# Cross-attention block: pair 4's turns back in step 4, norm1's turn of pair 3 at the end of step 5, the last pair's transfers on two queues, the last residual on VectorE

## The chip, the cores and the metric

The kernel runs on one core of a Trainium2 chip. The time is the device time of one execution in microseconds; lower is better. A core has five engines with queues of their own, which work in order: TensorE (PE in the profile; its weight loads are PEld), VectorE (DVE), ScalarE (ACT), GpSimd (POOL) and SyncE (SP). SP here does nothing but issue DMA transfers; ScalarE can issue some too. An engine waits for another, or for a transfer, on semaphores.

## The reference

A transformer block with strictly causal cross-attention, over 128 batches of 128 tokens, model width 256, 16 heads of 16, hidden width 1024, all in float32:

```python
q = (x @ Wq + bq);  k = (c @ Wk + bk);  v = (c @ Wv + bv)      # 16 heads of 16
scores = q @ k.T / sqrt(16);  allowed = j < i                   # strictly below the diagonal
attn = softmax(where(allowed, scores, -1e30));  attn[row 0] = 0
x1 = layer_norm(x + (attn @ v) @ Wo + bo, ln1_g, ln1_b)
out = layer_norm(x1 + relu(x1 @ W1 + b1) @ W2 + b2, ln2_g, ln2_b)
```

## The kernel before, in words

Two batches form a pair p, 0 to 63. The order on every engine is written out by hand: the kernel calls small functions, each of which records the instructions of one piece of work, and each engine runs its instructions in the order in which they were recorded. Software pipelining is done in this text. A step p holds the scores and the softmax of pair p, and beside them later stages of earlier pairs. `third()`, `fourth()`, `fifth()` and `fall_in(5)` are written out for p = 2, 3, 4, 5; `step(p)` serves 6 to 63; `behind(62)`, `behind(63)` and the lines after them empty the pipeline. Step numbers here are pair numbers.

The pieces that the change and the prediction name, with the lines of the kernel before:

- `scores_both` (L376) puts the scores in all eight PSUM banks; `mask` (L390), `mask_high` (L743, L747) and `low_maximum` (L754) run on VectorE, the exponentials on ScalarE (L762). `sums` adds up the rows on VectorE (L421) and multiplies by the reciprocals on GpSimd (L423).
- `turn(p, hi, t)` (L436) is a transpose of 32 x 32 blocks on VectorE, three for each pair: two for the upper half of the queries (hi = 1, t = 0 and 1) and one for the lower. They fill the tile tb. `bring` (L451) then moves tb's blocks to their places in the tile pT with 16 transfers of 96 KB; each of them reads what all three turns wrote. `LATE_FIRST` is the order of the 16.
- `weigh(p)` (L483, L493) multiplies pT with the values, into bank 7 (pc); `context` (L505) copies that out on ScalarE; `attention_out` (L512) multiplies with Wo; `attention_sum` (L538), `attention_stats` (L525, L526; L532, L533 on GpSimd), `shift` (L577) and `norm1` (L554, ScalarE) make x1.
- `turn_x1(p)` turns x1: a transpose on VectorE (L663) into tbx, then four transfers to DRAM (L239) and one back (L242) into x1T.
- `hidden(p)` (L699) multiplies x1T with W1 in four parts of two chunks; ScalarE applies the ReLU after each part (L707), and a function may be called between the parts. `residual1(p)` (L566, L569) makes x1b, the residual of the second half, on GpSimd.
- `combine_hidden` (L780 to L783) and `second_by_seven` (L794) multiply with W2 in seven products of quarter size instead of eight, into banks 6 and 7 (py, pz); `sum_of_seven` (L823, L831) adds them up with x1b on VectorE and frees the banks. Pairs 0 and 1 use `second` (L719) with `second_sum` (L729), pair 2 `second_half` (L840, sum L846).
- `norm2` (L591, ScalarE), `finish` (L597, L598, GpSimd) and `store` (L606, SP) end a pair; its tile t2 has two buffers, so that the sum of pair p waits for the store of pair p - 2.
- `load_ahead` issues the loads of x and c of coming pairs on SP (L92, L99).

In step p TensorE runs weigh(p - 2), scores(p), queries(p + 1), attention_out(p - 2), keys(p + 1), values(p), the product with W2 of pair p - 4 and hidden(p - 3). So step 6 begins with weigh(4), has second_half(2, 1) in the place of the product with W2, and ends with hidden(3).

Before the change, the first turn of pair 4 stands at the end of `fifth()`, its other two turns and the transfers in `fall_in(5)`, behind all masks of pair 5; on SP the store of pair 0 and the loads of `load_ahead(5)` stand ahead of those transfers. Pair 5 has its first two turns at the end of `fall_in(5)` and its third in step 6. `turn_x1(3)` stands in step 6 behind the third turn and the transfers of pair 5, on VectorE as on SP. In step 63, SP issues all 16 transfers of pair 63 and then store(58).

Of the kernel before, what the change touches and what calls it, by code (L numbers as in the profile page):

```python
# [19 lines left out]
def tile_cross_attention_block(  # L20
# [22 lines left out]
    nc = tc.nc  # L43
# [6 lines left out]
    FC = DFF // P  # L50
# [3 lines left out]
    NP = B // 2  # L54
# [162 lines left out]
    def bank(name):  # L217
        turns[0] += 1
        return at_bank(4 + turns[0] % 4, name)
# [210 lines left out]
    def turn(p, hi, t):  # L430

        st = states[p]
        if "tb" not in st:
            st["tb"] = wide(f"tb_{p}").rearrange("p (j n) -> p j n", j=NS)
        at = (t if hi else 2) * 256
        nc.vector.transpose(  # L436
            st["tb"][:, :, at : at + 256].rearrange("p j (n a) -> p n j a", a=32),
            st["sm", hi].rearrange("p h j -> p (h j)")[:, t * 1024 : (t + 1) * 1024].rearrange(
                "p (n j a) -> p n j a", j=NS, a=32
            ),  # L440
        )

    def bring(p, queue, which):

        st = states[p]
        if "pT" not in st:
            pT = st["pT whole"] = wide(f"pT_{p}").rearrange("p (i n) -> p i n", i=NS)
            st["pT"] = pT.rearrange("p i (n a) -> p i n a", a=32)
        for u in which:
            i, j = u // NS, u % NS  # L450
            queue.dma_start(  # L451
                st["pT whole"][32 * j : 32 * j + 32, i, :], st["tb"][32 * i : 32 * i + 32, j, :]
            )
# [49 lines left out]
    def context(p):  # L503
        pc = states[p].pop("pc").rearrange("p (u i) -> p u i", i=P)
        nc.scalar.copy(cxT.rearrange("p m s i -> p (m s) i")[:, :, 1:], pc[:, :, 1:])  # L505
# [53 lines left out]
                x1[:, s], t1[:, s], mv[:, s, 0:1], sd[:, s], ALU.subtract, ALU.mult  # L559
            )  # L560

    def residual1(p):

        st = states[p]
        x1b = st["x1b"] = ffn.tile([P, 2, D], F32, tag="x1b", name=f"x1b_{p}", bufs=3)
        nc.gpsimd.tensor_tensor(  # L566
            x1b, st["x1"], g1_r[:, None, :].to_broadcast([P, 2, D]), ALU.mult
        )
        nc.gpsimd.tensor_tensor(  # L569
            x1b, x1b, be1b_r[:, None, :].to_broadcast([P, 2, D]), ALU.add  # L570
        )

# [115 lines left out]
    def hidden(p, fs, between=None, banks=(2, 3, 4, 0)):  # L688
        st = states[p]
        if fs[0] == 0:  # L690
            st["hT"] = ffn.tile([P, FC, TP], F32, tag="hT", name=f"hT_{p}", bufs=1)
        for f in fs[::2]:
            if p == 0:
                ph = bank(f"ph_{p}_{f}")
            else:
                ph = at_bank(banks[f // 2], f"ph_{p}_{f}")
            for i in range(2):
                for k in range(KC):
                    nc.tensor.matmul(  # L699
                        ph[:, i * TP : (i + 1) * TP].rearrange("p (s i a) -> p s i a", s=2, a=32),  # L700
                        w1[:, k, (f + i) * P : (f + i + 1) * P], st["x1T"][:, :, :, k, :],
                        start=(k == 0), stop=(k == KC - 1),
                    )
                    if p == 1:
                        empty(3 if f else 2)
            for i in range(2):
                nc.scalar.activation(  # L707
                    st["hT"][:, f + i, :], ph[:, i * TP : (i + 1) * TP], AF.Relu,
                    bias=(b1e_c if p else b1_c)[:, f + i : f + i + 1], scale=1.0,
                )  # L710
            if between:
                between(f)
# [277 lines left out]
    EVERY = range(NS * NS)  # L990
# [52 lines left out]
    LATE_FIRST = (*EVERY[8:], *EVERY[:8])  # L1043
# [44 lines left out]
    def fifth():  # L1088
        p = 4
        load_ahead(p)  # L1090
        scores_both(p)
        mask(p, 0, B)
        mask(p, 1, A)
        maximum(p, 1, ONE)
        queries(p + 1)
        mask(p, 1, B)
        maximum(p, 1, TWO)
        exponential(p, 1, ONE)
        mask(p, 0, A)
        maximum(p, 0, ALL)  # L1100
        keys(p + 1)
        exponential(p, 1, TWO)
        values(p)
        values_out(p)
        sums(p, 1, ONE)
        exponential(p, 0, ALL)
        sums(p, 1, TWO)
        sums(p, 0, ALL)
        tokens(p + 2, "x")
        tokens(p + 2, "c")  # L1110
        second(1, 0)
        second(1, 1)
        combine_w2()
        turn(p, 1, 0)
        hidden(2, range(FC // 2))

    ONES, TWOS = range(HH), range(HH, H)
# [2 lines left out]
    def fall_in(p):  # L1120

        weigh(p - 2)
        context(p - 2)
        scores_both(p)
        second_sum(1)
        finish(0)
        store(0)
        add_bo(p - 1)
        residual1(2)
        load_ahead(p)  # L1130
        mask(p, 0, B)
        mask_high(p, A)
        exponential_by_head(p, 1, ONES)
        mask_high(p, B)
        exponential_by_head(p, 1, TWOS)
        mask(p, 0, A)
        low_maximum(p)
        turn(p - 1, 1, 1)
        turn(p - 1, 0, 0)
        bring(p - 1, nc.sync, LATE_FIRST)  # L1140
        queries(p + 1)
        exponential_by_head(p, 0, ONES)
        attention_out(p - 2)
        attention_sum(p - 2)
        attention_stats(p - 2)
        shift(p - 2, 1)
        project_keys(p + 1)
        values(p)
        sums(p, 1, ONE)
        sums(p, 1, TWO)  # L1150

        def between(f):
            if f == 4:
                exponential_by_head(p, 0, TWOS[:4])

        hidden(2, range(FC // 2, FC), between, (2, 3, 2, 3))
        exponential_by_head(p, 0, TWOS[4:])
        copy_keys(p + 1)
        values_out(p)
        norm1(p - 2)  # L1160
        tokens(p + 2, "x")
        tokens(p + 2, "c")
        turn(p, 1, 0)
        sums(p, 0, ALL)
        turn(p, 1, 1)
        second_half(2, 0)
        stats(1, states[1]["t2"], 2)
        scale_and_shift(1)

    def step(p):  # L1170
        last = p == NP - 1
        weigh(p - 2)
        context(p - 2)
        scores_both(p)
        if p > 6:
            combine_hidden(p - 4, POOL_ALONE)
        add_bo(p - 1)
        load_ahead(p)
        mask(p, 0, B)
        if last:  # L1180
            mask(p, 0, A)
        mask_high(p, A)
        exponential_by_head(p, 1, ONES)
        mask_high(p, B)
        exponential_by_head(p, 1, TWOS)
        if not last:
            mask(p, 0, A)
        low_maximum(p)
        exponential_by_head(p, 0, range(H))
        if p == 6:  # L1190
            turn(p - 1, 0, 0)
            bring(p - 1, nc.sync, LATE_FIRST)
            turn_x1(p - 3)
        if not last:
            queries(p + 1)
        attention_out(p - 2)
        attention_sum(p - 2)
        attention_stats(p - 2)
        shift(p - 2, 1)
        norm1(p - 2)  # L1200
        if not last:
            keys(p + 1)
        values(p)
        values_out(p)
        norm2(p - 5)
        sums(p, 1, ONE)
        sums(p, 1, TWO)
        sums(p, 0, ALL)
        turn_x1(p - 2)
        residual1(p - 3)  # L1210
        if p > 6:
            second_by_seven(p - 4)
        else:
            second_half(2, 1)
        hidden(p - 3, range(FC))
        if p + 2 < NP:
            tokens(p + 2, "x")
            tokens(p + 2, "c")
        turn(p, 1, 0)
        if p > 6:  # L1220
            sum_of_seven(p - 4)
        turn(p, 1, 1)
        turn(p, 0, 0)
        bring(p, nc.sync, LATE_FIRST)
        finish(p - 5)
        store(p - 5)
        stats(p - 4, states[p - 4]["t2"], 2)
        scale_and_shift(p - 4)
# [10 lines left out]
    def behind(p):  # L1239

        weigh(p)
        context(p)
        combine_hidden(p - 2, VECTOR_ALONE)
        norm2(p - 3)
        finish(p - 3)
        store(p - 3)
        second_by_seven(p - 2)
        attention_out(p)
        attention_sum(p)
        attention_stats(p)  # L1250
        shift(p, 1)
        residual1(p - 1)
        sum_of_seven(p - 2)
        stats(p - 2, states[p - 2]["t2"], 2)
        scale_and_shift(p - 2)
        hidden(p - 1, range(FC), lambda f: norm1(p) if f == 0 else None)
        turn_x1(p)

    p = NP - 1
# [1 line left out]
    behind(p - 1)  # L1261
    behind(p)
    combine_hidden(p - 1, VECTOR_ALONE)
    norm2(p - 2)
    second_by_seven(p - 1)
    residual1(p)
    finish(p - 2)
    store(p - 2)
    sum_of_seven(p - 1)
    hidden(p, range(FC))  # L1270
    stats(p - 1, states[p - 1]["t2"], 2)
    deviation(p - 1, 2)
    for s in range(2):
# [57 lines left out]
```

## Time and profile before

| what | us |
| --- | --- |
| median of 3 runs | 1552.5 (1551.95 to 1552.52) |
| the profiled execution | 1554.08 |
| its span, first to last instruction | 1552.4 |
| TensorE busy | 1518.0 (98%) |
| VectorE busy | 1334.9 (86%) |
| GpSimd busy | 1261.0 (81%) |
| ScalarE busy | 1121.2 (72%) |
| transfers | 204.24 MB, mean 132 GB/s |

The rows quoted in the prediction are of these kinds. A timeline row gives the start and the length in us, the engine, the line of the kernel, the operation, what it writes and reads, the shape and how many instructions are merged; in brackets stand the idle time of that engine just before, and what ended it. PE is a matmul; SPq and ACTq are transfers being issued by SP and by ScalarE. A row of waits gives who waited for whom, the sum in us, how often, and the longest. A row of stretches gives the busy time of each engine in a stretch of the span, and the granted clock of TensorE as a share of full speed. A row of the chain of work that ended last gives start, length and what ran.

### The profile page before, as it was taken

What the parts mean: (1) busy time and instruction counts of PE and PEld (TensorE: products, weight loads), DVE (VectorE), ACT (ScalarE), POOL (GpSimd) and SP (SyncE); (2) the same over time, 40 slices, a digit from 0 to 9 for tenths busy, and PEclk for the clock granted to TensorE, in tenths of its full rate; (3) what the DMA queues carried; (4) which work ended last, traced back from release to release, by engine and by line L of the source; (5) the groups of instructions that cost most, each with busy time, mean ns of one, the idle gap of its engine ahead of it and who ended that gap; (6) DMA issues with size and microseconds to landing.
All of it is one profiled execution on the core that took longest, in us unless ns stands there. A gap on an engine that the chain in (4) does not pass through costs nothing.

```text
span 1552.4 us, 47881 instructions
## 1 busy us (share of the span) xinstructions
PE 1518.0 (98%) x17926; PEld 1361.9 (88%) x17926; DVE 1334.9 (86%) x2496; ACT 1121.2 (72%) x3391; POOL 1261.0 (81%) x1284
## 2 busy tenths in 40 slices
PE   8995999999999999999999999999999999999998
PEld 7784898998998998998998998998998998998887
DVE  7987698898898898898898898898898898898875
ACT  5665587787787787787787787787787787787652
POOL 6875688888888888888888888888888888888873
PEclk9997999999999999999999999999999999999999
DMA  8445565565565565565566565566565566564431
GB/s 195 93 95 119 122 142 133 132 141 143 135 138 132 131 149 139 131 141 136 130 143 145 130 140 129 135 142 147 130 140 134 130 142 145 133 140 114 114 102 48
DMA packets 415285, 204.24 MB, mean 132 GB/s; under 512 B 282448, under 2 KB 383056, under 8 KB 415056
## 3 DMA queue, kind: packets, MB, share of 16 engines
q1 hardware_dynamic: 413152, 200.13, 56.1%
q8 instruction: 144, 2.36, 0.7%
q10 hardware_dynamic: 1904, 1.06, 0.3%
q14 instruction: 85, 0.70, 0.2%
HBM read 70.26 MB, written 33.29 MB: 67 GB/s over the span
## 4 chain that ended last, share of the span: by engine, by line
PE 92%; DVE 4%; DMA 2%; SPq 1%; issue 1%; ACT 1%; POOL 0%; ACTq 0%; POOLq 0%; DVEq 0%
PE ph L699 28%; PE py L794 13%; PE pz L794 10%; PE pq L261 7%; PE po L512 7%; PE pv L301 7%; PE pk L261 6%; PE pss L376 6%; PE pc L493 4%; PE pc L483 2%; SPq L451 1%; DVE su L421 1%; DMA x1T<-x1t 0%; PE py L719 0%; DMA pT<-tb 0%
## 5 line engine op out<-in xcount | busy, mean ns | idle before, releaser
L699 PE MATMUL ph<-x1T,w 128*128 128x256 f32 x2048 | 455.3, 380 | 12.8 <-DMA x1T<-x1t 12.7
L699 PEld LDWEIGHTS ph<-x1T,w 128*128 128x128 f32 x2048 | 385.4, 191 | 64.4 <-issue 13.2
L423 POOL TENSOR_TENSOR sm<-sm,rs 128x1024 f32<-128x1024 f32 x192 | 359.5, 1899 | 3.6 <-DVE rs L422 2.1
L707 ACT ACTIVATE hT<-ph,b1e_c 128x256 f32<-128x256 f32 x504 | 210.1, 469 | 189.2 <-PE ph L699 184.5
L762 ACT ACTIVATE sm<-pss,nmx 128x128 f32<-128x128 f32 x944 | 250.5, 416 | 127.3 <-DMA pT<-tb 85.2
L762 ACT ACTIVATE sm<-sm,nmx 128x64 f32<-128x64 f32 x944 | 232.2, 337 | 4.3
L390 DVE TENSOR_TENSOR sm<-pss,neg 128x256 f32<-128x256 f32 (+1 forms) x276 | 108.1, 434 | 146.6 <-PE pss L376 143.9
L421 DVE TENSOR_REDUCE su<-sm 128x8 f32<-128x1024 f32 (+1 forms) x192 | 225.8, 1176 | 3.9 <-ACT sm L409 3.8
L436 DVE STREAM_TRANSPOSE tb<-sm 128x1024 f32<-128x1024 f32 x186 | 221.1, 1214 | 0.0
L532 POOL TENSOR_SCALAR ve<-mv 128x2 f32<-128x2 f32 x127 | 28.9, 228 | 210.4 <-DVE mv L526 210.1
L794 PE MATMUL py<-wt,hS 128*128 128x128 f32 x1440 | 171.1, 275 | 1.0 <-DVE hS L782 0.5
L794 PEld LDWEIGHTS py<-wt,hS 128*128 128x128 f32 x1440 | 165.8, 192 | 1.4 <-DVE hS L782 0.7
L747 DVE TENSOR_REDUCE nmx<-pss 128x4 f32<-128x512 f32 x236 | 150.7, 680 | 0.0
L261 PE MATMUL pq<-xT,wq 128*128 128x256 f32 x504 | 125.4, 392 | 0.5 <-DVE sm L390 0.5
L291 ACT ACTIVATE kT<-pk,bkh,half 128x256 f32<-128x256 f32 x252 | 120.6, 559 | 3.9 <-PE pk L261 3.9
L512 PE MATMUL po<-wo,cxT 128*128 128x256 f32 x512 | 121.3, 380 | 0.7 <-ACT cxT L505 0.7
L301 PE MATMUL pv<-wv,cT 128*128 128x256 f32 x512 | 121.0, 379 | 0.0
L261 PE MATMUL pk<-cT,wk 128*128 128x256 f32 x504 | 119.2, 379 | 0.0
L512 PEld LDWEIGHTS po<-wo,cxT 128*128 128x128 f32 x512 | 96.9, 190 | 14.4 <-ACT cxT L505 1.2
L261 PEld LDWEIGHTS pq<-xT,wq 128*128 128x128 f32 x504 | 90.7, 189 | 20.8 <-issue 9.9
L301 PEld LDWEIGHTS pv<-wv,cT 128*128 128x128 f32 x512 | 97.2, 190 | 13.2
L261 PEld LDWEIGHTS pk<-cT,wk 128*128 128x128 f32 x504 | 95.7, 190 | 13.1 <-issue 0.2
(133 smaller groups left out, 2976.7 us busy)
## 6 DMA issues: line engine op xcount, KB each, us to landing
pT<-tb SPq DMA_DIRECT2D x984, 96.0 KB
x1t<-tbx SPq DMA_DIRECT2D x252, 64.0 KB
x1T<-x1t SPq DMA_DIRECT2D x63, 256.0 KB
out_dram<-t SPq DMA_DIRECT2D x63, 256.0 KB
xb<-in_x_dram SPq DMA_DIRECT2D x124, 128.0 KB
cb<-in_ctx_dram SPq DMA_DIRECT2D x124, 128.0 KB
x<-in_x_dram SPq DMA_DIRECT2D x31, 512.0 KB
w<-in_L_xattn_W_dram SPq DMA_DIRECT2D x2, 1024.0 KB
```

Source lines behind the costliest of these rows:

```text
L261: nc.tensor.matmul(ps[:, m * TP : (m + 1) * TP], w[:, k, m * P : (m + 1) * P], src[:, k, :], start=(k == 0), stop=(k == KC - 1),)
L291: nc.scalar.activation(st["kT"][:, m, e, :], pk[:, m * TP : (m + 1) * TP], AF.Identity, bias=bkh[:, m, e : e + 1], scale=half[:, e : e + 1],)
L301: nc.tensor.matmul(pv[:, s * D : (s + 1) * D], st["cT"][:, k, s * P : (s + 1) * P], wv[:, k, :], start=(k == 0), stop=(k == KC - 1),)
L421: nc.vector.tensor_reduce(su, sm[:, part, :], AX.X, ALU.add)
L423: nc.gpsimd.tensor_tensor(sm[:, part, :], sm[:, part, :], rs[:, :, None].to_broadcast([P, part.stop - part.start, n]), ALU.mult,)
L436: nc.vector.transpose(st["tb"][:, :, at : at + 256].rearrange("p j (n a) -> p n j a", a=32), st["sm", hi].rearrange("p h j -> p (h j)")[:, ...
L512: nc.tensor.matmul(po[:, s * D : (s + 1) * D], cxT[:, k, s, :], wo[:, k, :], start=(k == 0), stop=(k == KC - 1),)
L699: nc.tensor.matmul(ph[:, i * TP : (i + 1) * TP].rearrange("p (s i a) -> p s i a", s=2, a=32), w1[:, k, (f + i) * P : (f + i + 1) * P], st[ ...
L707: nc.scalar.activation(st["hT"][:, f + i, :], ph[:, i * TP : (i + 1) * TP], AF.Relu, bias=(b1e_c if p else b1_c)[:, f + i : f + i + 1], sc ...
L747: nc.vector.tensor_reduce(st["nmx", 1][:, 4 * r : 4 * r + 4], st["sps", 1][r].rearrange("p (n j) -> p n j", j=P), AX.X, ALU.max, negate=True,)
L762: nc.scalar.activation(sm[:, h, :], src, AF.Exp, bias=nmx[:, h : h + 1], scale=1.0)
L794: nc.tensor.matmul(out, left(k), right(k), start=(k == 0), stop=(k == FC // 2 - 1))
```

## The change

Four things, all of them order, queue or engine; the computation is the same.

1. The second and third turn of pair 4 and its 16 transfers move from `fall_in(5)` to `fifth()`, behind the first turn.
2. `turn_x1(3)` moves from the middle of step 6 to `fall_in(5)`, behind the second turn of pair 5 and ahead of `second_half(2, 0)`.
3. Of the 16 transfers of pair 63, the first eight of the order stay with SP in step 63; the other eight are issued by ScalarE in `behind(62)`, after `context(62)`.
4. `residual1(63)` runs on VectorE. `sum_of_seven(62)` follows it at once, `norm2(61)` is called after the first part of `hidden(63)`, and `finish(61)` and `store(61)` come after `hidden(63)`.

In the built program the sequence of matmuls on TensorE is the same before and after.

```diff
-    def residual1(p):
+    def residual1(p, engine=nc.gpsimd):
...
-        nc.gpsimd.tensor_tensor(
+        engine.tensor_tensor(
             x1b, st["x1"], g1_r[:, None, :].to_broadcast([P, 2, D]), ALU.mult
         )
-        nc.gpsimd.tensor_tensor(
+        engine.tensor_tensor(
             x1b, x1b, be1b_r[:, None, :].to_broadcast([P, 2, D]), ALU.add
         )
...
         turn(p, 1, 0)
+        turn(p, 1, 1)
+        turn(p, 0, 0)
+        bring(p, nc.sync, LATE_FIRST)
         hidden(2, range(FC // 2))
...
         low_maximum(p)
-        turn(p - 1, 1, 1)
-        turn(p - 1, 0, 0)
-        bring(p - 1, nc.sync, LATE_FIRST)
         queries(p + 1)
...
         turn(p, 1, 1)
+        turn_x1(p - 2)
         second_half(2, 0)
...
             bring(p - 1, nc.sync, LATE_FIRST)
-            turn_x1(p - 3)
...
-        bring(p, nc.sync, LATE_FIRST)
+        bring(p, nc.sync, LATE_FIRST[: len(EVERY) // (1 + last)])
...
         context(p)
+        if p == NP - 2:
+            bring(p + 1, nc.scalar, LATE_FIRST[len(EVERY) // 2 :])
         combine_hidden(p - 2, VECTOR_ALONE)
...
     combine_hidden(p - 1, VECTOR_ALONE)
-    norm2(p - 2)
     second_by_seven(p - 1)
-    residual1(p)
+    residual1(p, nc.vector)
+    sum_of_seven(p - 1)
+    hidden(p, range(FC), lambda f: norm2(p - 2) if f == 0 else None)
     finish(p - 2)
     store(p - 2)
-    sum_of_seven(p - 1)
-    hidden(p, range(FC))
```

## The prediction

> **What bounds the kernel now.** First the page: which engine carries the chain of work that ended last, and how full is it?
>
> ```profile
> span 1552.4 us, 47881 instructions
> PE 1518.0 (98%) x17926; PEld 1361.9 (88%) x17926; DVE 1334.9 (86%) x2496; ACT 1121.2 (72%) x3391; POOL 1261.0 (81%) x1284
> PE 92%; DVE 4%; DMA 2%; SPq 1%; issue 1%; ACT 1%; POOL 0%; ACTq 0%; POOLq 0%; DVEq 0%
> ```
>
> TensorE (PE) is the bound, so only time in which it stands still or runs slowly can be won. Then the waits of TensorE, longest first, to find where that is:
>
> ```profile
> PE ph L699 <- DMA x1T<-x1t: 12.7, 1, 12.7
> PE pc L483 <- DMA pT<-tb: 6.7, 1, 6.7
> ```
>
> Two single waits, 19.4 us in all. The timeline of TensorE shows where they sit, and what a step costs without them:
>
> ```profile
> 128.30 0.65 PE L483 MATMUL pc<-pT,vd 128*32 128x64 f32 x16 [6.69 <-DMA pT<-tb]
> 133.29 1.99 PE L261 MATMUL pq<-xT,wq 128*128 128x256 f32 x8
> 140.31 3.62 PE L840 MATMUL py<-w,hT 128*128 128x256 f32 x16
> 156.60 8.75 PE L699 MATMUL ph<-x1T,w 128*128 128x256 f32 x32 [12.68 <-DMA x1T<-x1t]
> 165.28 0.43 PE L483 MATMUL pc<-pT,vd 128*32 128x64 f32 x16
> ...
> 188.57 0.43 PE L483 MATMUL pc<-pT,vd 128*32 128x64 f32 x16
> 191.60 1.99 PE L261 MATMUL pq<-xT,wq 128*128 128x256 f32 x8
> 198.61 1.05 PE L794 MATMUL py<-w,hT 128*128 128x128 f32 x8
> 204.86 7.07 PE L699 MATMUL ph<-x1T,w 128*128 128x256 f32 x32
> 211.87 0.43 PE L483 MATMUL pc<-pT,vd 128*32 128x64 f32 x16
> ```
>
> Both waits are in step 6, which the change touches: weigh(4) waits for pT of pair 4, hidden(3) for x1T of pair 3. From 188.57 on a step takes 23.30 us without a wait. The same stretches are slower in step 6: weigh and scores took 133.29 - 128.30 = 4.99 us against 191.60 - 188.57 = 3.03, hidden 8.68 against 7.01. The clock says why:
>
> ```profile
> 142.81:146.22 3.41, 1.11 (x6) 0.63 (x4) 3.31 (x7) 3.06 (x8) 3.31 (x5) 1.00 0.62 146
> 146.22:149.63 3.41, 0.00 (x0) 0.00 (x0) 3.41 (x7) 2.67 (x7) 3.41 (x3) 0.50 0.66 160
> 1504.71:1508.12 3.41, 2.12 (x63) 1.65 (x65) 3.20 (x8) 1.34 (x4) 0.67 (x1) 1.00 0.00 0
> ```
>
> (Stretch, length, busy PE, PEld, DVE, ACT, POOL, then the granted clock.) In the second wait the clock falls to 0.50, and the slow stretches say the same of the first: each wait costs a cold stretch besides, 1.96 and 1.67 us.
>
> **The change part by part: the seam of steps 4 to 6.** What held the two transfers, in the queue of SP and on the engines that feed it:
>
> ```profile
> 116.40 10.10 SPq L451 DMA_DIRECT2D pT<-tb  x16
> 139.93 10.11 SPq L451 DMA_DIRECT2D pT<-tb  x16
> 150.14 1.99 SPq L239 DMA_DIRECT2D x1t<-tbx  x4
> ```
>
> ```profile
> 125.88 0.18 DVE L526 BATCH_NORM_AGGREGATE mv<-bs 128x2 f32<-128x6 f32 x1
> 132.29 0.76 DVE L390 TENSOR_TENSOR sm<-pss,neg 128x256 f32<-128x256 f32 x2 [6.22 <-PE pss L376]
> 138.63 1.23 DVE L436 STREAM_TRANSPOSE tb<-sm 128x1024 f32<-128x1024 f32 x1
> ```
>
> ```profile
> 97.42 5.62 POOL L423 TENSOR_TENSOR sm<-sm,rs 128x1024 f32<-128x1024 f32 x3
> 122.99 1.09 ACT L554 ACTIVATE x<-t,nb,sd 128x256 f32<-128x256 f32 x2
> ```
>
> Pair 4. VectorE's two further turns (some 1.15 us each, row 138.63) now follow the first one in step 4. Their input is ready when GpSimd's last product ends at 103.04, so they end near 105.3 instead of the middle of step 5. VectorE waits there for the scores of pair 5, and second_sum(1) behind the turns ends near 106, so I cost that at nothing; without that cover it would be 2.3 us. The 16 transfers go past SP's store(0) and the loads of c and x, and run from 105.4 to 115.5. From first issue to weigh took 128.30 - 116.40 = 11.90 us, so pT is there at 117.3; TensorE arrives at 128.30 - 6.69 = 121.6. The wait of 6.69 goes. The store and the loads are 5 us later; they are first used in step 6 or 7. Step 5 loses 2.3 us of turns on VectorE ahead of attention_sum(3); that wins nothing, because norm1(3) stands behind other work of ScalarE.
>
> Pair 3. turn_x1(3) moves ahead of second_half(2, 0). It needs norm1(3), ScalarE's last work of step 5, done at 124.08, so its turn, half the size of that in row 138.63, ends near 124.7. From SP's first issue to hidden took 156.60 - 150.14 = 6.46 us, so x1T is there at 131.3, with SP free by then; the loads of x that now stand behind it end near 131.5, before SP's next job. What waits behind it on VectorE: the sum of second_half(2, 0), which frees its bank for the last of pair 6's scores, the statistics, and all masks of pair 6. The old end of the statistics, 126.06, moves by 0.1 to 126.2, and the masks start there, no longer at 132.29. TensorE therefore stalls some 2 us between 124 and 126.6 (bank of the sum, then the mask in front of queries). From queries: 7.02 us to second_half(2, 1) (133.29 to 140.31), 3.6 for it: hidden(3) at 137.1, 5.8 us after its x1T. The wait of 12.68 goes too. TensorE ends hidden(3) at 137.1 + 7.0 = 144.1.
>
> What is late next: weigh(5). Its transfers start behind pair 5's last turn, which still stands behind the masks of pair 6: 139.93 - 132.29 = 7.64 us after these start, so at 133.8, and pT is there 11.90 later, at 145.7. So 1.6 us of waiting are left, and weigh(5) starts at 145.7, not 165.28: **19.5 us won**. Bounds: 16 transfers took 11.68 us beside other transfers (row 187.82 below) against 10.1, so at worst 1.6 us less; if pT were in time, 144.1 and 1.6 more. Cold stretches are taken as zero; at the other end one of 1.7 to 2.0 us comes after the remaining wait. The clock fell after a window with 1.11 of 3.41 us busy and not after one with 2.12; a wait of 1.6 us inside one window leaves 1.8 busy, nearer to the latter, so I take no drop. [...]
>
> From step 7 on nothing changes in the order. SP's queue, the tightest, has room to take the earlier start:
>
> ```profile
> 187.82 11.68 SPq L451 DMA_DIRECT2D pT<-tb  x16
> SPq L451 <- DVE bs L525: 121.6, 52, 3.7
> ```
>
> The second row is SP's own waits between 200 and 1400 us: 2.3 us a step in which SP waits for VectorE.
>
> **The end.**
>
> ```profile
> 1507.35 0.43 PE L483 MATMUL pc<-pT,vd 128*32 128x64 f32 x16 [1.29 <-issue]
> 1517.20 7.17 PE L699 MATMUL ph<-x1T,w 128*128 128x256 f32 x32
> 1524.21 1.22 PE L794 MATMUL py<-w,hT 128*128 128x128 f32 x8
> 1532.92 7.07 PE L699 MATMUL ph<-x1T,w 128*128 128x256 f32 x32
> ```
>
> ```profile
> 1504.47 0.69 DVE L823 TENSOR_TENSOR t<-x1b,py 128x512 f32<-128x512 f32 x1 [3.38 <-DMA out_dram<-t]
> 1509.65 0.68 DVE L781 TENSOR_TENSOR hS<-hT 128x512 f32<-128x512 f32 x1
> 1526.78 1.75 DVE L781 TENSOR_TENSOR hS<-hT 128x512 f32<-128x512 f32 x1
> 1526.38 1.59 POOL L569 TENSOR_TENSOR x1b<-x1b,be1b_r 128x512 f32<-128x512 f32 x1
> 1491.28 10.58 SPq L451 DMA_DIRECT2D pT<-tb  x16
> 1526.89 0.38 SPq L242 DMA_DIRECT2D x1T<-x1t  x1
> 1512.58 4.58 DMA x1T<-x1t
> L451 ACTq DMA_DIRECT2D pT<-tb x8: 597/602/612, 61.7 to 66.2; - x8
> ```
>
> Last pair's transfers. SP issued all 16 until 1501.9, and store(58) behind them; the sum of pair 60 waited 3.38 us for that store's buffer, and weigh(63) 1.29 us for the bank this sum reads (it ended at 1507.2). With 8 transfers on ScalarE's queue, SP is done near 1497, the store lands near 1500, and the sum starts right behind VectorE's statistics at 1501.1. ScalarE pays 8 x 0.64 = 5.1 us of issue from 1491.7 to about 1497; behind it stands norm2(59), 1.5 us later than now, and ScalarE has nothing else until 1501. The 1.29 us go, with a little of the wait before hidden(62): 1.5, between 0 (if weigh is held by something else) and 1.6.
>
> Last residual on VectorE. The second combination of pair 62 took 1.75 us beside GpSimd's residual1(63), whose own instruction took 1.59; the combination of pair 61 in row 1509.65 took 0.68. The four together held second_by_seven(62): it took 1532.92 - 1524.21 = 8.71 us against 204.86 - 198.61 = 6.25 in a step. Both GpSimd jobs leave this place: residual1 goes to VectorE behind the combinations, finish(61) behind norm2(61), which now stands after the first part of hidden(63). So 8.71 becomes 6.3: **2.4 us won**, between 0 and 2.5. The two new VectorE instructions are priced by 1509.65 (0.68 each; at worst 1.75) and lie under second_by_seven, before the sum that needs its end: nothing. norm2(61) takes 1.09 of ScalarE between two hidden parts: nothing, there is about 0.9 us of room in each. finish(61) now ends near 1535.5 and delays pair 62's deviation on GpSimd, so its norm ends near 1538, 1.5 us before VectorE is needed for py_last. x1T(63) was issued at 1526.89 and would be at 1525.4; the transfer has 3.6 us until hidden(63) at 1529.0. That of pair 62 took 4.58 us in the chain, that of pair 3 at most 156.60 - 150.14 - 1.99 = 4.5 with its first half, so I take it as in time; up to 1.0 could be lost.
>
> **Sum.** 19.5 + 1.5 + 2.4 = 23.4 us. The profiled execution took 1554.1 us with a span of 1552.4, so 1.7 lie around it; the median is 1552.5. 1552.5 - 23.4 = **1529.1 us** (span 1529.0).
>
> **The rivals.**
> The clock drops after all (at the 1.6 us before weigh(5), or at the stall near 125): the window row with 1.11 busy speaks for it, the one with 2.12 against; 1529.1 + 1.8 = 1530.9. [...]
> The end gives nothing, because x1T(63) or the store binds: 1529.1 + 3.9 = 1533.0. Against it: the store would have to land 1 us later than the sum's other inputs, and x1T(63) 3.6 us after its issue.
> pT(5) comes later than worked out, its transfers slowed by the x1T and loads ahead: 11.68 for 10.1, with a cold stretch: 1529.1 + 1.6 + 1.8 = 1532.5.
> Only pair 4's wait goes and x1T(3) stays late because its turn waits on VectorE or SP: 1552.5 - 6.7 - 2.0 - 3.9 = 1539.9. Against it: 5.8 us of room.
> Slower than before: SP, which now starts pair 6 against a TensorE that is 19.5 us further, cannot keep up, and weigh waits in every step. It decides from 23.4 / 57 steps = 0.41 us a step on; at 0.8 us the time is 1552.5 - 23.4 + 45.6 = 1574.7. Against it stand SP's 2.3 us a step.
>
> **How the numbers follow.** Forecast 0.58, clock 0.17, end 0.07, late pT(5) 0.08, x1T(3) 0.04, slower 0.04, no net change 0.02. The range reaches from pT(5) in time (1529.1 - 1.6, and 0.9 for small terms: 1526.6) to both the end failing and a small loss more: 1534.0; that leaves out the last three cases, 1 in 10, and what I have not seen. 0.2% (3 us) is what a measurement here can tell from no change. Faster 0.94, same 0.02, slower 0.04.
>
> **What would show it.** In the profile after: no wait of hidden(3) for x1T; weigh(4) without a wait for pT, 16 transfers issued from about 105.4; weigh(5) at about 145.7 with a wait of 1 to 2.5 us for pT; steps of 23.3 us from there; no wait for out_dram in front of the sum of pair 60; combinations of pair 62 at 0.7 us each and second_by_seven(62) at 6.3. Wrong would be: a wait over 3 us in steps 5 to 7, a step longer than 23.3, or hidden(63) waiting for x1T.

## The result and the profile after

The changed kernel takes 1531.6 us (median of 4 runs, 1530.83 to 1532.31), against 1552.5: a ratio of 0.9866, with a 95% interval of 0.9849 to 0.9883. Timed once more beside other kernels it took 1533.6 (4 runs, 1531.65 to 1535.02; before there 1552.5), a ratio of 0.9873 (0.986 to 0.9887). Its profiled execution took 1530.83 us with a span of 1529.2; that of before took 1554.08 with 1552.4. The difference of the spans, 23.2 us, can be followed row by row.

From the page, the span, the busy times and the chain that ended last:

```profile
span 1529.2 us, 47881 instructions
PE 1513.2 (99%) x17926; PEld 1358.5 (89%) x17926; DVE 1332.5 (87%) x2498; ACT 1120.4 (73%) x3391; POOL 1257.2 (82%) x1282
PE 93%; SPq 2%; DVE 2%; DMA 1%; issue 1%; ACT 1%; POOL 0%; ACTq 0%; POOLq 0%; DVEq 0%
```

The waits of TensorE (sum, times, longest). The waits of before, 12.7 us of hidden(3) for x1T and 6.7 us of weigh(4) for pT, are gone; a new one of 2.1 us for pT stands at weigh(5):

```profile
PE pc L483 <- DMA pT<-tb: 2.1, 1, 2.1
PE pq L261 <- DVE sm L390: 1.2, 2, 1.0
PE pss L376 <- DVE t L846: 0.6, 1, 0.6
```

The timeline of TensorE at the seam, from second_half(2, 0) on:

```profile
117.54 3.62 PE L840 MATMUL py<-w,hT 128*128 128x256 f32 x16
121.09 0.43 PE L483 MATMUL pc<-pT,vd 128*32 128x64 f32 x16
...
124.74 0.67 PE L376 MATMUL pss<-kT,qT 32*64 32x128 f32 x16 [0.61 <-DVE t L846]
126.42 1.99 PE L261 MATMUL pq<-xT,wq 128*128 128x256 f32 x8 [1.02 <-DVE sm L390]
...
136.89 7.07 PE L699 MATMUL ph<-x1T,w 128*128 128x256 f32 x32
146.09 0.43 PE L483 MATMUL pc<-pT,vd 128*32 128x64 f32 x16 [2.13 <-DMA pT<-tb]
...
169.38 0.43 PE L483 MATMUL pc<-pT,vd 128*32 128x64 f32 x16
```

What feeds it, on SP and on VectorE:

```profile
104.92 11.59 SPq L451 DMA_DIRECT2D pT<-tb  x16
...
124.40 1.87 SPq L239 DMA_DIRECT2D x1t<-tbx  x4
128.16 3.21 SPq L92 DMA_DIRECT2D xb<-in_x_dram  x4
133.56 10.84 SPq L451 DMA_DIRECT2D pT<-tb  x16
```

```profile
101.41 3.45 DVE L436 STREAM_TRANSPOSE tb<-sm 128x1024 f32<-128x1024 f32 x3
...
123.66 0.71 DVE L663 STREAM_TRANSPOSE tbx<-x 128x512 f32<-128x512 f32 x1 [1.49 <-ACT x L554]
124.30 0.39 DVE L846 TENSOR_TENSOR t<-py,x1b 128x256 f32<-128x256 f32 x1
...
125.94 0.76 DVE L390 TENSOR_TENSOR sm<-pss,neg 128x256 f32<-128x256 f32 x2 [0.19 <-DMA x1t<-tbx]
```

Weigh(4) (121.09) and hidden(3) (136.89) wait for nothing. The kernel before had second_half(2, 0) at 118.00 and weigh(5) at 165.28; these two rows, and one of the end, were not shown yet:

```profile
118.00 3.62 PE L840 MATMUL py<-w,hT 128*128 128x256 f32 x16
...
1489.43 0.43 PE L483 MATMUL pc<-pT,vd 128*32 128x64 f32 x16
```

So this stretch shrank from 47.28 us to 146.09 - 117.54 = 28.55: **18.73 won**. It started 0.46 earlier than before. That lead is there at 33.53 us already (the first product with Wo, at 33.99 before), ahead of every edit, so it isn't the change's, and I count every later place by its distance from second_half(2, 0). From weigh(5) to weigh(6) passed 23.29 us, as before (188.57 - 165.28), and from weigh(6) to weigh(62) 1300.85 us (1300.86 before).

The end, on TensorE, VectorE and ScalarE. The sum of pair 60 (1481.81) no longer waits for a store, and a combination of pair 62 takes 0.72 us:

```profile
1470.23 0.43 PE L483 MATMUL pc<-pT,vd 128*32 128x64 f32 x16
...
1486.79 0.43 PE L483 MATMUL pc<-pT,vd 128*32 128x64 f32 x16
...
1496.35 7.07 PE L699 MATMUL ph<-x1T,w 128*128 128x256 f32 x32
1503.26 1.22 PE L794 MATMUL py<-w,hT 128*128 128x128 f32 x8
...
1509.67 7.07 PE L699 MATMUL ph<-x1T,w 128*128 128x256 f32 x32
```

```profile
1481.81 0.68 DVE L823 TENSOR_TENSOR t<-x1b,py 128x512 f32<-128x512 f32 x1
...
1504.33 0.72 DVE L780 TENSOR_TENSOR hS<-hT 128x512 f32<-128x512 f32 x1 [1.20 <-ACT hT L707]
...
1520.23 0.42 DVE L1287 TENSOR_TENSOR t_last<-py_last,x1b 128x256 f32<-128x256 f32 x1 [1.52 <-PE py_last L1283]
```

```profile
1472.51 6.09 ACTq L451 DMA_DIRECT2D pT<-tb  x8
1478.72 1.09 ACT L591 ACTIVATE t<-t,nb,sd 128x256 f32<-128x256 f32 x2 [6.24 <-DMA pT<-tb]
```

Weigh(62) to weigh(63) took 16.56 us (17.92 before), from there to the product with W2 16.47 (16.86), and second_by_seven(62) 6.41 (8.71): 1.36 + 0.39 + 2.30 = **4.05 won**. 0.46 + 18.73 + 4.05 = 23.2, the whole difference of these two executions.

### The profile page after: what moved, and what is told of

Its sections match the earlier page's. It is cut to its first block, busy times and chain, and to the rows that moved or that the text cites. A ratio compares the mean times of both kernels' runs of the same rounds, so it can differ in the third digit from the quotient of the medians.

```text
span 1529.2 us, 47881 instructions
## 1 busy us (share of the span) xinstructions
PE 1513.2 (99%) x17926; PEld 1358.5 (89%) x17926; DVE 1332.5 (87%) x2498; ACT 1120.4 (73%) x3391; POOL 1257.2 (82%) x1282
## 3 DMA queue, kind: packets, MB, share of 16 engines
q10 hardware_dynamic: 2288, 1.85, 0.5%
## 4 chain that ended last, share of the span: by engine, by line
PE 93%; SPq 2%; DVE 2%; DMA 1%; issue 1%; ACT 1%; POOL 0%; ACTq 0%; POOLq 0%; DVEq 0%
PE ph L699 27%; PE py L794 14%; PE pz L794 11%; PE pq L261 7%; PE po L512 7%; PE pv L301 7%; PE pk L261 7%; PE pss L376 6%; PE pc L493 4%; PE pc L483 2%; SPq L451 2%; DMA pT<-tb 0%; PE ptp L466 0%; DVE sm L390 0%; DVE su L421 0%
```

## The experiments

Most of these kernels were timed once; they are compared by the same stretches of their traces, not by those single times. "Before" and "the changed kernel" are the two shown above.

**Each half of the seam alone.** The kernel before with part 1 of the change only:

```diff
         turn(p, 1, 0)
+        turn(p, 1, 1)
+        turn(p, 0, 0)
+        bring(p, nc.sync, LATE_FIRST)
...
-        turn(p - 1, 1, 1)
-        turn(p - 1, 0, 0)
-        bring(p - 1, nc.sync, LATE_FIRST)
```

> The kernel before with only the first edit: the turns and transfers of pair 4 in step 4. Theory (each move takes away its own wait, but turn_x1(3) still stands behind pair 5's third turn and its 16 transfers): no wait at weigh(4), the masks of pair 6 start near 126, pair 5's transfers run from 133.8 to 144.6, the transfers of x1 follow, and hidden(3) starts 6.5 us later, near 151, after a wait of some 14 us. So 5.5 us of the 8.7 (wait and cold stretch) of weigh(4) arrive at hidden(3): about 1547. Rival 1 (the waits are independent): all 8.7 us, about 1544. Rival 2 (the wait for x1T takes back all): no change, 1552.5.

It took 1547.05 us. Second_half(2, 0) stands at 118.40, and in its timeline:

```profile
132.21 10.12 SPq L451 DMA_DIRECT2D pT<-tb  x16
148.84 9.45 PE L699 MATMUL ph<-x1T,w 128*128 128x256 f32 x32 [12.63 <-DMA x1T<-x1t]
158.22 0.43 PE L483 MATMUL pc<-pT,vd 128*32 128x64 f32 x16
```

To weigh(5) it is 39.82 us: 7.46 won, though the wait of hidden(3) is as long as before. With weigh(4) on time the scores and masks of pair 6 came earlier, and with them pair 5's last turn and its transfers (132.21, 8.1 us earlier by the distance from second_half(2, 0)) and all that stood behind them on SP, x1T(3) included. Hidden(3) started 8.16 us earlier than before by that distance and took 0.70 us longer itself (9.45 against 8.75, and 7.07 in a step without a wait). That more of the cold stretch lies in it is my estimate from these lengths. The expectation was 5.5 us, or 8.7 if the two waits were independent; 7.46 is nearer to the second. The wait for x1T did not grow by what weigh(4) gained, because its transfers came earlier by as much.

The kernel before with part 2 only:

```diff
         turn(p, 1, 1)
+        turn_x1(p - 2)
         second_half(2, 0)
...
-            turn_x1(p - 3)
```

> The kernel before with only the second edit: turn_x1(3) at the end of step 5. Theory: weigh(4) waits 6.7 us as before, hidden(3) waits for nothing and starts near 144, pair 5's transfers run from 139.9 to 150.0 or 150.7, and weigh(5) starts near 152 with a wait of about 1 us for pT: 165.3 - 152 = 13.3 us, about 1539. With pair4_alone this adds up to the 19 us of both. Rival 1 (the move only swaps the waits: pair 5's transfers, now behind x1's on SP, come as late as x1T did): no more than 3 us, about 1550. Rival 2 (the front of step 6 gives nothing without pair 4's move): 1552.5.

1539.52 us, second_half(2, 0) at 117.67:

```profile
127.67 0.65 PE L483 MATMUL pc<-pT,vd 128*32 128x64 f32 x16 [6.39 <-DMA pT<-tb]
...
142.95 7.07 PE L699 MATMUL ph<-x1T,w 128*128 128x256 f32 x32
151.69 0.43 PE L483 MATMUL pc<-pT,vd 128*32 128x64 f32 x16 [1.68 <-DMA pT<-tb]
```

34.02 us to weigh(5): 13.26 won. That is what was expected (13.3): the wait for x1T goes without part 1. Together the parts won 18.73, not 7.46 + 13.26 = 20.72: both advance the same chain, and what is left is the wait for pair 5's transfers.

**The split of the last pair's transfers.** The changed kernel with all 16 on SP:

```diff
-        bring(p, nc.sync, LATE_FIRST[: len(EVERY) // (1 + last)])
+        bring(p, nc.sync, LATE_FIRST)
...
-        if p == NP - 2:
-            bring(p + 1, nc.scalar, LATE_FIRST[len(EVERY) // 2 :])
```

> The changed kernel with all 16 transfers of the last pair on SP again. Theory: store(58) is issued behind them, the sum of pair 60 waits some 3.4 us for it, weigh(63) waits 1.3 us for the bank, and hidden(62) starts 1.5 us later: the end is 1.5 to 1.6 us later than in the changed kernel, and all before step 63 is as there. Rival (the bank or the store was not what held weigh(63)): no wait before weigh(63), no loss.

1533.12 us. VectorE's sum of pair 60, and weigh(63) behind it:

```profile
1486.18 0.69 DVE L823 TENSOR_TENSOR t<-x1b,py 128x512 f32<-128x512 f32 x1 [3.51 <-DMA out_dram<-t]
```

```profile
1489.06 0.43 PE L483 MATMUL pc<-pT,vd 128*32 128x64 f32 x16 [1.42 <-issue]
```

Both waits are back, and weigh(62) to hidden(63) takes 40.94 us instead of 39.44: the split is worth 1.50.

**The residual, and finish(61).** Two kernels take the two GpSimd jobs apart. The first has residual1(63) on GpSimd again, in the new order:

```diff
-    residual1(p, nc.vector)
+    residual1(p)
```

> The changed kernel with the last residual on GpSimd again, its place in the order kept and finish(61) behind hidden(63). Theory (each GpSimd job slows the combinations only while it runs): residual1(63) runs beside the first two combinations of pair 62, which take 1.0 to 1.7 us, the last two take 0.7, and second_by_seven(62) is 0.4 to 0.8 us longer than 6.4; the rest of the 2.4 us came from finish(61). Rival 1 (residual1 alone cost it): second_by_seven(62) back to 8.7, 2.3 us lost. Rival 2 (the order alone won it): no loss.

The second leaves it on VectorE and puts norm2(61), finish(61) and store(61) back:

```diff
     combine_hidden(p - 1, VECTOR_ALONE)
+    norm2(p - 2)
     second_by_seven(p - 1)
     residual1(p, nc.vector)
+    finish(p - 2)
+    store(p - 2)
     sum_of_seven(p - 1)
-    hidden(p, range(FC), lambda f: norm2(p - 2) if f == 0 else None)
-    finish(p - 2)
-    store(p - 2)
+    hidden(p, range(FC))
```

> The changed kernel with norm2(61), finish(61) and store(61) back at their old place; residual1(63) stays on VectorE. Against the changed kernel, second_by_seven(62) took 8.71 us before and 6.41 after, and 7.09 with residual1(63) alone back on GpSimd. Theory A, one slack used once: the combinations have some 1 us of room before the matmuls that read them, so the two instructions of finish(61), like the two of residual1(63), cost 0.4 to 1.1 us when they run alone beside them, and only all four together cost 2.3: second_by_seven(62) takes 6.8 to 7.5 us. Theory B, additive: finish(61) alone makes up the rest, 2.3 - 0.7 = 1.6 us, and it takes 8.0. Theory C: finish(61) has no part, the rest came from norm2(61) or from something else of the kernel before: 6.4. L781 to L783 beside GpSimd should read about 1.7 us each, and 0.7 where GpSimd has nothing.

They took 1533.89 and 1531.98 us. VectorE and GpSimd in the second:

```profile
1505.74 0.68 DVE L781 TENSOR_TENSOR hS<-hT 128x512 f32<-128x512 f32 x1
1506.34 1.75 DVE L782 TENSOR_TENSOR hS<-hS,hT 128x512 f32<-128x512 f32 x1
1508.13 1.65 DVE L783 TENSOR_TENSOR hS<-hT,hS 128x512 f32<-128x512 f32 x1
```

```profile
1506.26 1.29 POOL L597 TENSOR_TENSOR t<-t,g_r 128x512 f32<-128x512 f32 x1 [0.98 <-ACT t L591]
1507.62 1.60 POOL L598 TENSOR_TENSOR t<-t,be_r 128x512 f32<-128x512 f32 x1
```

Each pair of GpSimd instructions slowed two of the four combinations, by some 1.05 us each, and the others stayed at 0.7. Second_by_seven(62) took 7.09 us with residual1(63) there (0.68 more than 6.41), 6.77 with finish(61) there (0.36 more), and 8.71 before, with both (2.30 more). So the two do not add up, as theory A had it (its 6.8 to 7.5 us is just missed); the first text had expected that finish(61) makes up the rest.

The end of before does not always cost the same. The two kernels with one half of the seam have it too: second_by_seven(62) took 8.96 us in the one with pair 4's move, and 7.88 in the one with turn_x1(3) moved, where the first combination started at 1511.49, 0.15 us ahead of GpSimd's first instruction, and took 0.73, so that three were slowed and not four. Both jobs together thus cost 1.47 to 2.55 us in three executions, in each more than the 0.36 + 0.68 of the two alone.

The last combination has room: in the changed kernel it ends at 1506.97, and its product starts at 1508.78, so 1.8 us later. Two slowed combinations (+2.0 to 2.1) use that up and lose 0.2 to 0.3 more, three (+3.1) lose 1.3, four (+3.9: 1.57, 1.75, 1.75 and 1.64 us before, for 2.77 together) lose 2.1; the measured losses are 0.36 and 0.68, 1.47, and 2.30. The 0.68 lies furthest off: with residual1(63) on GpSimd the matmuls wait for the third combination (0.41 us), not for the last.

In these rows the two engines end by turns: GpSimd's first instruction at 1507.55, the combination of 1506.34 at 1508.09, GpSimd's second at 1509.22, the last combination at 1509.78. The steps are 0.54, 1.13 and 0.56 us, near what a combination (0.68) and a GpSimd instruction (1.27) took alone.

**The changed kernel timed again.** No edit.

> The changed kernel once more. Theory (what is left of the wait at weigh(5), 1.5 to 2.7 us, sometimes costs a cold stretch of TensorE and sometimes not, by where the gate's window falls): weigh(5) to weigh(6) takes 23.3 us in some runs and 24.6 in others, and the times fall into groups some 1.4 us apart, near 1531 and 1532.3. Rival (the groups come from the length of the wait itself, from the transfers): 23.3 us in all, the wait differs by 1.4 us.

What that text calls the gate's window are the stretches of 3.41 us on which the clock changed in the traces (below). The kernel took 1533.6 us (median), with a span of 1531.2 in the profile. The seam to weigh(5) is the same (28.59 us), but weigh(5) to weigh(6) took 171.42 - 146.56 = 24.86 us instead of 23.29. The timeline and the stretches before and after the end of the wait (PE, PEld, DVE, ACT, POOL, then the granted clock):

```profile
146.56 0.66 PE L483 MATMUL pc<-pT,vd 128*32 128x64 f32 x16 [2.17 <-DMA pT<-tb]
...
171.42 0.43 PE L483 MATMUL pc<-pT,vd 128*32 128x64 f32 x16
```

```profile
143.17:146.58 3.41, 1.24 (x9) 0.79 (x9) 3.01 (x6) 2.27 (x7) 3.33 (x3) 1.00 0.63 151
146.58:149.99 3.41, 3.41 (x119) 3.24 (x125) 0.00 (x0) 0.53 (x1) 3.06 (x7) 0.50 0.30 72
```

The clock fell to 0.50 for one window: the cold stretch that the clock rival foresaw, 1.57 us. The kernel with the residual on GpSimd shows it too (24.62 us from weigh to weigh, 1.33 more). In four other profiles with this wait it does not occur, and it isn't the length of the wait that decides:

```profile
146.83 0.43 PE L483 MATMUL pc<-pT,vd 128*32 128x64 f32 x16 [2.44 <-DMA pT<-tb]
```

This is the row of the kernel with finish(61) at its old place: a wait of 2.44 us at full clock, where 2.17 cost a cold stretch.

What differs is where the wait lies. In these traces the clock changed on a grid: it fell at 27.12 and at 146.58 us in this trace, at 27.14 and 146.61 in the one with the residual on GpSimd, and at 26.75, 125.73 and 146.21 before. The cold stretch near 27 us lasts 3.41 us in each of these, and the later falls came a whole number of such stretches after it (35, 35, and 29 and 35). If windows of 3.41 us are laid from the fall near 27 us in each trace, the one in which TensorE worked least around weigh(5) is this:

| kernel | wait at weigh(5), us | window | TensorE busy in it | clock in the next |
| --- | --- | --- | --- | --- |
| changed kernel | 2.13 | 141.67 to 145.09 | 2.29 | 1.00 |
| the same again | 2.17 | 143.17 to 146.58 | 1.24 | 0.50 |
| residual on GpSimd | 2.70 | 143.19 to 146.61 | 1.18 | 0.50 |
| finish(61) at its old place | 2.44 | 142.77 to 146.19 | 1.62 | 1.00 |
| all 16 transfers on SP | 2.38 | 142.52 to 145.94 | 1.90 | 1.00 |
| sum ahead (below) | 2.21 | 143.81 to 147.23 | 2.07 | 1.00 |
| turn_x1(3) alone | 1.68 | 148.63 to 152.04 | 1.74 | 1.00 |

In these seven traces the waits that left TensorE 1.24 us of work or less in one window cost a cold stretch; those that an edge divided so that each window kept 1.62 or more did not. The times did not fall into two groups 1.4 us apart, as the text expected; the start of the kernel varies by more than that (last section).

**Closing what is left of the seam.** Three kernels go on from the changed one. The first moves the sum ahead of the turn of x1:

```diff
-        turn_x1(p - 2)
         second_half(2, 0)
         stats(1, states[1]["t2"], 2)
+        turn_x1(p - 2)
```

> The changed kernel with the sum of second_half(2, 0) and the statistics of pair 1 ahead of turn_x1(3) on VectorE. Theory (turn_x1(3) waits for ScalarE and holds VectorE's work behind it): the sum and the statistics fill that wait, the masks of pair 6 start 1.5 us earlier, the stalls of 0.6 and 1.0 us in scores and before queries go, pair 5's transfers start 1.5 us earlier, and weigh(5) starts 1.5 us earlier after the same wait of some 2 us. Rival (the masks are held by TensorE's scores): less than 0.5 us.

It took 1532.88 us, since it reached second_half(2, 0) only at 121.16 (last section); from there to weigh(5) took 26.93 us, 1.62 less than in the changed kernel (1.5 expected), and to weigh(6) as well. The two stalls at 124.74 and 126.42 in the changed kernel, 1.63 us, are what it took away: scores(6) no longer waits for the sum.

The second starts pair 5's last turn and transfers, in step 6, ahead of the last masks of pair 6, and puts the loads behind them:

```diff
-        load_ahead(p)
+        if p != 6:
+            load_ahead(p)
...
         exponential_by_head(p, 1, ONES)
+        if p == 6:
+            turn(p - 1, 0, 0)
+            bring(p - 1, nc.sync, LATE_FIRST)
         mask_high(p, B)
...
         low_maximum(p)
+        if p == 6:
+            load_ahead(p)
         exponential_by_head(p, 0, range(H))
-        if p == 6:
-            turn(p - 1, 0, 0)
-            bring(p - 1, nc.sync, LATE_FIRST)
```

> The changed kernel with pair 5's third turn between the two halves of pair 6's high masks, and its transfers ahead of load_ahead(6). Theory (the transfers of pair 5 are what weigh(5) waits for): they start near 129.8 and end near 140.5, pT is there at 142.3, before TensorE comes at 143.9; the wait of 2.1 us goes, weigh(5) starts 2.1 us earlier, with no cold stretch. Rival (the second half of the masks, 1.2 us later, holds ScalarE's exponentials and through their banks values or hidden): part of it comes back as a wait before values(6) or hidden(3).

1530.39 us. Weigh(5) comes 26.34 us after second_half(2, 0), 2.21 less, and waits for nothing. Of that 0.77 comes back in the next step (24.06 us), as the rival had it, if at another place: the scores of pair 7 find the banks of hidden(3) not yet read by ScalarE. The profile names 0.28 us of it as a wait.

```profile
144.83 0.43 PE L483 MATMUL pc<-pT,vd 128*32 128x64 f32 x16
...
147.10 1.59 PE L376 MATMUL pss<-kT,qT 32*64 32x256 f32 x56 [0.28 <-ACT hT L707]
```

Both together:

> Both of these edits. Theory: TensorE runs from step 5 into step 7 without a wait over 0.5 us, weigh(5) starts near 142.4, 3.7 us earlier than in the changed kernel: 1527.3 if all else is as there, and the cold stretch of step 7 cannot come, so the times lie closer together. Rival (pT of pair 5 or ScalarE's exponentials bind next): 2 to 3 us only.

1528.2 us (1526.19 to 1531.51, 5 runs), a ratio of 0.9841 (0.9828 to 0.9855) to the kernel before, below the 0.9873 (0.986 to 0.9887) of the changed kernel in the same comparison. Weigh(5) comes after 24.65 us, weigh(6) 24.09 later: by these stretches 3.90 - 0.80 = 3.1 us are won, while the medians are 5.4 apart. The times do not lie closer together, as the text expected; they spread over 5.3 us, with no cold stretch in the trace.

Then norm2(1), which stands ahead of the ReLU of hidden(3) on ScalarE, goes behind it:

```diff
-        norm2(p - 5)
+        if p > 6:
+            norm2(p - 5)
...
         hidden(p - 3, range(FC))
+        if p == 6:
+            norm2(p - 5)
```

> The changed kernel with both of the moves ahead (second_half(2, 0) and its statistics ahead of turn_x1(3); third turn and transfers of pair 5 two exponentials earlier, the loads of step 6 behind the masks), and with norm2(1) of step 6 behind hidden(3) on ScalarE instead of ahead of it. With the two moves alone, the step from weigh(5) to weigh(6) took 24.09 us instead of 23.29, since scores(7) waited for ScalarE's ReLU of hidden(3), which stands behind norm2(1) (1.09 us). Theory A, that ScalarE is late by that much: the ReLU ends 1.0 earlier, the wait of 0.3 to 0.8 us goes, the step takes 23.3 and the median is 0.8 below that of the two moves alone (1528.2): 1527.4. Rival B: the ReLU waits for the matmuls of hidden(3) themselves or for another engine, or the wait returns as context(5) behind norm2(1): 24.1 and 1528.2. Rival C: finish(1) and store(1), 1 us later, make something later in step 7 late: over 1528.2.

1527.3 us (1525.86 to 1528.80, 5 runs), a ratio of 0.9831 (0.9816 to 0.9846). In its trace weigh(5) still comes 24.65 us after second_half(2, 0), and the step after takes 23.60 us, 0.49 less than with the two moves alone:

```profile
117.47 3.62 PE L840 MATMUL py<-w,hT 128*128 128x256 f32 x16
...
142.12 0.43 PE L483 MATMUL pc<-pT,vd 128*32 128x64 f32 x16
...
165.72 0.43 PE L483 MATMUL pc<-pT,vd 128*32 128x64 f32 x16
```

So ScalarE was late, as theory A says, but 0.3 of the 0.8 us stay, with no wait in the trace that explains them. They lie in the scores of pair 7, which take 1.85 us to the first matmul of queries against 1.55 in the changed kernel. The times of the last two kernels, which are from two comparisons, overlap; only the trace tells them apart, and that the median is near the expected 1527.4 says little. Both are faster than the changed kernel.

## Why the prediction was right, and where it was off

**Pair 4.** As worked out: the turns end at 104.86, the 16 transfers start at 104.92 (105.4 on the clock of before, as predicted), weigh(4) doesn't wait. They took 11.59 us to issue instead of 10.10, which cost nothing.

**Pair 3.** On the clock of before (0.46 added) the turn ended at 124.83 (124.7 predicted), the masks of pair 6 started at 126.40 (126.2), and the stall of "some 2 us" is 0.61 + 1.02 = 1.63. Hidden(3) started at 137.35 (137.1) without a wait.

**What is late next.** It is weigh(5), with a wait of 2.13 us where I had 1.6. The mis-sized term is the 16 transfers of pair 5: 10.84 us, between my 10.1 and my bound of 11.68, right behind the four x1t transfers and the loads. From first issue to weigh passed 12.53 us instead of 11.90. With the masks 0.2 us later, weigh(5) stands at 146.55 on the clock of before instead of 145.7, and the gain is 18.73, not 19.5.

**The clock.** "I take no drop" holds for the profiled execution and not for all. The argument was sound for the wait that it was made for: 1.6 us leave at least 1.8 us of work in any window of 3.41, and no window with 1.62 or more at this place was followed by a drop. But the wait was 2.13, by the mis-sized transfers, and a wait of that length cost a cold stretch or not by how it lay on the windows; that it cost none in the profiled execution is luck. A wait of 2.44 us went without a drop, one of 2.17 did not. The clock fell there after a window that was busy for 1.24 of 3.41 us, and in the kernel before after one with 1.11.

**The end.** 4.05 instead of 3.9. Split: 1.50 by experiment, 1.5 predicted. ScalarE's 8 transfers took 6.09 us instead of 5.1, so norm2(59) came later than I had it, at 1478.72, but TensorE did not wait for it. Residual and finish(61): 2.30, predicted 2.4; "the four together" was the right reading, since either job alone would have cost only 0.36 to 0.68. The 2.4 was read from one execution; against the two others with the same end it is 1.47 and 2.55. X1T(63) was in time: hidden(63) starts 0.89 after the last product, with no wait, 3.32 us after the transfer was issued at 1506.35. That was not worked out: the two rows that I cited had 4.58 and 4.5 us, more than the 3.6 us of room. The norm of pair 62 left 1.52 us of room at 1520.23, as worked out. The 0.39 us between weigh(63) and the product with W2 belong to the execution of before rather than to the change: there the weight load of hidden(62) waited 0.53 us for x1T, and the kernel with turn_x1(3) alone, whose end is that of before, has the same 16.47 us as the changed one. From weigh(62) to hidden(63) the three executions with the end of before took 43.49, 43.34 and 42.46 us, so the 39.44 of the changed kernel are worth 3.02 to 4.05.

**Slower than before.** SP kept up. In its own waits between 200 and 1400 us there is as much room as before:

```profile
SPq L451 <- DVE bs L525: 117.9, 51, 3.2
```

**The level.** Span against span the forecast is 0.2 us off (1529.0, measured 1529.2). Part of that is luck: the seam gave 0.8 less than forecast, the end 0.15 more, and the 0.46 of the start, which no edit made, nearly closes the gap. The medians are 2.5 and 4.5 above 1529.1. I had taken the gain from a profiled execution that was 1.6 us slower than the median of before, and subtracted it from that median. If the typical run of before paid less in its two cold stretches than the profiled one (1.96 and 1.67), the typical gain is smaller too; there is only one trace of before, so this stays open. The cold stretch after the wait, 1.3 to 1.6 us in two of the six profiles of kernels with both parts of the seam and this wait, is another part in the second comparison, but not in the first: its two longer runs (1532.3) show a mean granted clock of 1.000 and the two shorter ones (1530.8 and 1530.9) 0.998, so a cold stretch is not what set them apart. The start of the kernel (last section) could be; three of these four runs have no trace, so this stays open too.

## What to carry to other kernels

When a wait on a chain of turns and transfers is taken away, ask for the next chain that starts from the same place, and price its transfers by a row in which they stand behind others, not by the fastest row (here 10.84 us, where I had 10.1). Work that slows an engine beside it costs nothing until the room ahead of its reader is used up, and then all of it (here 1.8 us of room: 2.0 to 2.1 us of slowing cost 0.36 and 0.68, and 3.9 cost 2.30): count the room first, and don't price such jobs one by one. A forecast of the clock holds only for the wait that it was made for: ask what a wait half a microsecond longer would cost (here 1.6 us forecast, 2.13 measured, and 1.57 more in one execution). Subtract a gain from the execution that it was read from, and add what the other runs differ in as a range.

## What the runs showed of the hardware

A wait of 2.1 to 2.7 us cost 1.3 to 1.6 us more, or nothing, even in two executions of one program, by its place on windows of 3.41 us. At weigh(5) the clock fell after windows in which TensorE was busy for 1.18 and 1.24 us, and stayed after 1.62 and more; near 27 us it fell after 1.12 to 1.60.

The start varies too: second_half(2, 0) was reached at 117.47 us in one kernel (norm2(1) behind hidden(3)) and at 121.16 in the one with the sum ahead, though no edit stands before it. Of these 3.7 us, 2.4 are there at the second group of transposes (L466), which starts at 26.23 in the one and at 28.59 in the other. In the second the eight matmuls of the first keys (L874) took 3.78 us, against 1.99 in the changed kernel (L466 at 26.28), though the profile shows no lower clock there. The rest is the clock, which fell near 27 us in both, for 3.41 us in the first and for twice that, 27.76 to 34.59, in the second:

```profile
27.40:30.80 3.40, 2.21 (x11) 2.24 (x12) 3.37 (x5) 1.90 (x6) 3.40 (x2) 0.55 0.90 99
30.80:34.20 3.40, 3.40 (x75) 2.74 (x77) 1.49 (x5) 2.48 (x4) 3.13 (x3) 0.50 0.79 121
```

In ten traces the first keys were read: they took 1.99 to 2.07 us in six and 3.75 to 3.78 in four. The other two (norm2(1) behind hidden(3), and finish(61) at its old place) have L466 at 26.23 and 26.54, as the six have it at 26.28 to 26.57. Three of the four have no cold stretch near 27 us and reach second_half(2, 0) at 118.40 to 118.62. So up to 3.7 us of difference are there before the change begins. Runs of the kernel before spread as widely (1551.05 to 1556.05 in one comparison), so a single time doesn't tell parts of 1 to 2 us apart here, and the stretches of the trace do.
